# A selective scan on Trainium2: every second state's input term made tokens-first by ScalarE and turned by TensorE into PSUM

## The chip, the cores and the metric

One core of a Trainium2 chip runs the whole kernel. Its engines work side by side, each through its own queue in order: TensorE (PE; its weight loads are listed as PEld) multiplies matrices into PSUM, VectorE (DVE) and ScalarE (ACT) work element by element, GpSimd (POOL) issues the gathers, SyncE (SP) issues the other DMAs. The metric is the device time of one launch in microseconds (us).

## What is computed

Two layers on an image tensor of 4 x 128 x 128 x 128 (batch, height, width, channels), each added to its input after a group norm:

```
x = x + L0(gn(x))      # deformable convolution, two groups, nine taps
x = x + L1(gn(x))      # two Mamba blocks on rows of 128 tokens

def mamba_block(h):                      # d = 256 channels, n = 16 states
    u, res = split(h @ in_w)
    u      = silu(causal_conv4(u) + cb)
    dt, Bm, Cm = split(u @ xw)           # 8, 16, 16
    delta  = softplus(dt @ dtw + dtb)
    A      = -exp(A_log)
    # for every token t, channel d and state n:
    #   h[t] = exp(delta[t,d] * A[d,n]) * h[t-1] + delta[t,d]*u[t,d]*Bm[t,n]
    #   y[t,d] = sum_n h[t,d,n] * Cm[t,n]
    return ((y + u * Dp) * silu(res)) @ ow
```

The change concerns the recurrence over t alone: its decay `exp(delta*A)`, its input term `delta*u*B`, and the product with C. All is in 32-bit floats.

## The kernel before

Layer 0 (`layer0`, from line 420) gathers corners of a table with indirect DMAs (line 364, `gt`, four buffers), multiplies them by bilinear weights on VectorE (line 382, `gw`, two buffers), turns and sums them on TensorE into a bank `p4` of the pool `ps`, copies that to SBUF with ScalarE (line 396, `s`), and adds the taps up in PSUM (line 415, `acc`).

Layer 1 works on blocks of four sequences of 128 tokens (512 tokens), with channels on the partitions, 256 channels being NC = 2 tiles of 128. For each block and Mamba layer there are two parts:

- `pre` makes the projections: `u` (matmuls line 501 into two `ps1` tiles, Silu line 508), the gate `g` (513, 518), B, C and dt (`pdb` 521, `dbl` 524, sent to DRAM as `bcd` 526), then for each channel tile `pdt` (534), Abs, Exp, add and Ln on ScalarE (538 to 546) and two VectorE steps (547, 548) for softplus, and last `delta` (549) and `delta*u` (`du`, 550).
- `main` runs eight steps of two states (NQ = 2). A step broadcasts two rows of B and two of C to all partitions by DMA (570), clears the first column of each sequence's decays on ScalarE (575), makes four exponentials of 127 tokens in four sequences (580), multiplies `du` by B for each state (586, two products of 1024), runs one scan over 2 x 2 x 512 elements (592) that leaves the states in the decay tile `da` (three such tiles in turn), multiplies them by C (596, one product of 2048), and turns them on TensorE, adding into PSUM `y` (line 604, through the helper at 128). After the last step y is multiplied by the gate (607), turned back (`pyg`, 612, copied by 613) and projected (`pout`, 617 or 624 and 626, copied by 619 or 630).

`main` of a job is emitted after `pre` of the next job. Jobs go in the order block a layer 0, block b layer 0, block a layer 1, block b layer 1, then the next pair, so that the `pre` that runs under a `main` needs at most the output of the job before that `main`. There are 256 jobs. `u` has one buffer, so a `pre` can begin only when `main` of the job before it has started and read the old one (561).

The first image's layer 0 runs alone. Then a loop at the end (lines 661 to 668) deals out steps of layer 1 of one image and units of layer 0 of the next, and the last image's layer 1 runs alone. The order on each engine is set by a scheduler at compile time: it takes ready instructions in program order, a tile from a pool only when a buffer is free, and adds the semaphores. So the number of buffers of a pool shapes the order of every queue. PSUM has eight banks: `ps` 2, `psa` 2, `ps1` 2, and `y` 2.

The pools at lines 92 to 97 and `pre` and `main` are what the change touches. The helper that turns and adds is one line:

```
nc.tensor.matmul(o, v, ident, is_transpose=True, start=start, stop=stop, skip_group_check=True)
```

Of the kernel before, what the change touches and what calls it, by code (L numbers as in the profile page):

```python
# [10 lines left out]
F32 = mybir.dt.float32  # L11
# [6 lines left out]
P = 128  # L18
# [45 lines left out]
def block_kernel(ctx: ExitStack, tc: tile.TileContext, a: dict, out: bass.AP):  # L64
# [26 lines left out]
    pb = ctx.enter_context(tc.tile_pool(name="l0b", bufs=1))  # L91
    ps = ctx.enter_context(tc.tile_pool(name="l0ps", bufs=2, space=PSUM))
    psa = ctx.enter_context(tc.tile_pool(name="l0psa", bufs=2, space=PSUM))
    p2 = ctx.enter_context(tc.tile_pool(name="l1p2", bufs=1))
    pd = ctx.enter_context(tc.tile_pool(name="l1d", bufs=3, space=DRAM))
    ps1 = ctx.enter_context(tc.tile_pool(name="l1ps", bufs=2, space=PSUM))
    psy = ctx.enter_context(tc.tile_pool(name="l1psy", bufs=1, space=PSUM))

    def loadw(name, shape, src=None, pool=cw, tag=None):
        t = pool.tile(shape, F32, name=f"w_{name}", tag=tag) if tag else pool.tile(shape, F32, name=f"w_{name}")  # L100
        nc.sync.dma_start(t, a[name] if src is None else src)
        return t
# [32 lines left out]
    dw = loadw("dw", [P, NT, NT], pool=p2, tag="dbl")  # L135
    dwb = loadw("dwb", [P, NT], pool=p2, tag="ot")
    pw = loadw("pw", [P, NT, CG], pool=p2, tag="u")
# [19 lines left out]
    nc.vector.tensor_scalar(aneg, aneg, -1.0, None, ALU.mult)  # L157
    dpar = loadw("dpar", [P, NL, NC], pool=p2, tag="ot")
    for l in range(NL):
        for c in range(NC):  # L160
            nc.vector.tensor_scalar(ddiag[:, l, c, :], ident, dpar[:, l, c : c + 1], None, ALU.mult)
    inw = loadw("inw", [P, NL, NC * P], a["inw"][:, :, 0 : NC * P], pool=p2, tag="yg")
    cvw = loadw("cvw", [P, NL, DCONV, NC * P], pool=p2, tag="hs")
    for l in range(NL):
        nc.vector.tensor_tensor(
            inc[:, l], cvw[:, l], inw[:, l].unsqueeze(1).to_broadcast([P, DCONV, NC * P]), ALU.mult
        )
# [293 lines left out]

    NDA = 3
    das = [cw.tile([P, NC, NQ, SR, P], F32, name=f"da{i}") for i in range(NDA)]
    zero = cw.tile([P, NC * NQ * SR], F32, name="zero")
    nc.vector.memset(zero, 0.0)
    n_da = [0]
# [17 lines left out]
    def pre(st, l):  # L484
# [65 lines left out]
        nc.vector.tensor_tensor(du, de, u, ALU.mult)  # L550
        st.update(u=u, g=g, delta=de, du=du, bcd=bcd)

    def main(st, l):
# [5 lines left out]
        for i in range(SR):  # L559
            for c in range(NC):  # L560
                nc.tensor.matmul(  # L561
                    y[:, i, c], st["u"][:, c, i * P : (i + 1) * P], ddiag[:, l, c, :],
                    start=(i % 2 == 0 and c == 0), stop=False, skip_group_check=True,
                )
        for q in range(NS // NQ):
            bc = []
            for w in range(2):
                t = p2.tile([P, NQ, TB], F32, tag=f"bc{w}", name=f"bc{w}_{nm}_{q}", bufs=2)
                n0 = w * NS + q * NQ
                nc.sync.dma_start(t, st["bcd"][n0 : n0 + NQ, :].partition_broadcast(P))  # L570
                bc.append(t)
            da = das[n_da[0] % NDA]
            n_da[0] += 1

            nc.scalar.copy(da.rearrange("p c n s t -> p (c n s) t")[:, :, 0], zero)
            for c in range(NC):
                dv = st["delta"][:, c].rearrange("p (s t) -> p s t", s=SR)
                for n in range(NQ):
                    s = q * NQ + n
                    nc.scalar.activation(  # L580
                        da[:, c, n, :, 1:], dv[:, :, 1:], AF.Exp, scale=aneg[:, l, c, s : s + 1]
                    )
            hs = p2.tile([P, NC, NQ, TB], F32, tag="hs", name=f"hs_{nm}_{q}")

            for n in range(NQ):
                nc.vector.scalar_tensor_tensor(  # L586
                    hs[:, :, n, :], st["du"], ones[:, 0:1],
                    bc[0][:, n].unsqueeze(1).to_broadcast([P, NC, TB]),
                    op0=ALU.mult, op1=ALU.mult,
                )  # L590
            df = da.rearrange("p c n s t -> p (c n s t)")
            nc.vector.tensor_tensor_scan(  # L592
                df, df, hs.rearrange("p c n t -> p (c n t)"), zero[:, 0:1], ALU.mult, ALU.add
            )
            dc = da.rearrange("p c n s t -> p c (n s t)")
            nc.vector.scalar_tensor_tensor(  # L596
                dc, dc, ones[:, 0:1],
                bc[1].rearrange("p n t -> p (n t)").unsqueeze(1).to_broadcast([P, NC, NQ * TB]),
                op0=ALU.mult, op1=ALU.mult,
            )  # L600
            for c in range(NC):
                for n in range(NQ):
                    for i in range(SR):
                        add_transposed(y[:, i, c], da[:, c, n, i, :], False, q == NS // NQ - 1 and n == NQ - 1)
            yield
# [14 lines left out]
        else:  # L620
            x1t = load_x1(blk, f"o{nm}")
            for i in range(SR):
                o = po[:, i * P : (i + 1) * P]
                nc.tensor.matmul(o, x1t[:, i * P : (i + 1) * P], ident, start=True, stop=False)
                for c in range(NC):
                    nc.tensor.matmul(
                        o, yg[:, c, i * P : (i + 1) * P], ow[:, l, c, :], start=False, stop=(c == NC - 1)
                    )
            ot = p2.tile([P, SR, P], F32, tag="ot", name=f"ot_{nm}")
            nc.scalar.copy(ot.rearrange("p r c -> p (r c)"), po)  # L630
# [117 lines left out]
```

## Time and profile before

| what | value |
|---|---|
| median of three runs | 26672.16 us (26664.46 to 26679.19) |
| profiled execution, its own time | 26698.06 us |
| its span | 26696.0 us |
| busy: VectorE | 23505.8 us, 88% |
| busy: TensorE, weight loads | 19620.5 us, 73%; 13523.4 us, 51% |
| busy: GpSimd | 16017.0 us, 60% |
| busy: ScalarE | 11605.1 us, 43% |
| HBM traffic | 142 GB/s over the span |

A profile lists, for each engine, how long it was busy, in the whole span or in a stretch of it, and in groups of like instructions: line, engine, operation, output <- inputs, shapes and count, then busy time, mean duration of one in ns, and the idle time of the engine just before them with what ended it. A wait shown there is the engine's own: whoever stands behind it in its queue waits too. A share of the whole span mixes stages with different limits, so stages are read one by one.

### The profile page before, as it was taken

What the parts mean: (1) busy time and instruction counts of PE and PEld (TensorE: products, weight loads), DVE (VectorE), ACT (ScalarE), POOL (GpSimd) and SP (SyncE); (2) the same over time, 40 slices, a digit from 0 to 9 for tenths busy, and PEclk for the clock granted to TensorE, in tenths of its full rate; (3) what the DMA queues carried; (4) which work ended last, traced back from release to release, by engine and by line L of the source; (5) the groups of instructions that cost most, each with busy time, mean ns of one, the idle gap of its engine ahead of it and who ended that gap; (6) DMA issues with size and microseconds to landing.
All of it is one profiled execution on the core that took longest, in us unless ns stands there. A gap on an engine that the chain in (4) does not pass through costs nothing. (4 is left out here: it accounts for less than half of the span.)

```text
span 26696.0 us, 294801 instructions
## 1 busy us (share of the span) xinstructions
PE 19620.5 (73%) x112196; PEld 13523.4 (51%) x112196; DVE 23505.8 (88%) x14042; ACT 11605.1 (43%) x18181; POOL 16017.0 (60%) x9222
## 2 busy tenths in 40 slices
PE   4777788878888778887888778888888655555555
PEld 3444455555555555555555555555555443434344
DVE  2232289999999999999999999999999999999999
ACT  0000044444444544444444454444445455555554
POOL 4777777878877767888878667877878400000000
PEclk7888888888999888888998888899998866666666
DMA  5363344456544444455544444444444333333332
GB/s 146 114 172 107 106 147 155 157 170 183 165 153 154 149 144 155 158 173 181 164 154 153 148 143 151 156 150 152 154 154 156 130 107 106 107 106 107 107 106 102
DMA packets 1994602, 3804.53 MB, mean 143 GB/s; under 512 B 771796, under 2 KB 1116116, under 8 KB 1993053
## 3 DMA queue, kind: packets, MB, share of 16 engines
q1 hardware_dynamic: 1550812, 2577.13, 29.9%
q0 software_dynamic: 442368, 1208.55, 14.4%
q8 instruction: 880, 14.42, 0.2%
q14 instruction: 542, 4.43, 0.0%
HBM read 3567.63 MB, written 217.05 MB: 142 GB/s over the span
## 5 line engine op out<-in xcount | busy, mean ns | idle before, releaser
L364 POOL DMA_INDIRECT gt<-table,idx x9216 | 16016.3, 1738 | 5031.5 <-issue 2999.5
L592 DVE TENSOR_TENSOR_SCAN da<-da,zero,hs 128x2048 f32<-128x2048 f32 x2048 | 9176.1, 4481 | 351.7 <-ACT da L580 247.1
L128 PE MATMUL y<-ident,da 128*128 128x128 f32 x32768 | 5252.0, 326 | 3956.1 <-DVE da L596 3955.4
L580 ACT ACTIVATE da<-de,aneg 128x508 f32<-128x508 f32 x8192 | 5550.5, 712 | 5605.2 <-PE y L128 5351.0
L128 PEld LDWEIGHTS y<-ident,da 128*128 128x128 f32 x32768 | 4682.4, 171 | 4953.3 <-DVE da L596 2520.6
L415 PE MATMUL acc<-s,wc 128*64 128x256 f32 (+3 forms) x38400 | 6403.2, 453 | 761.4 <-ACT s L396 760.9
L586 DVE SCALAR_TENSOR_TENSOR hs<-du,ones,bc 128x1024 f32<-128x1024 f32 x4096 | 5093.2, 1277 | 0.0
L415 PEld LDWEIGHTS acc<-s,wc 128*64 128x64 f32 x38400 | 3352.0, 145 | 3083.2 <-issue 1446.2
L596 DVE SCALAR_TENSOR_TENSOR da<-da,ones,bc 128x2048 f32<-128x2048 f32 x2048 | 4807.9, 2348 | 25.9
L382 DVE TENSOR_TENSOR gw<-gt,wt 128x1024 f32<-128x1024 f32 x2304 | 2786.4, 1213 | 2133.3 <-DMA gt<-table,idx 1500.9
L128 PE MATMUL p<-ident,gw 128*128 128x128 f32 x18432 | 2724.3, 299 | 1714.1 <-DVE gw L382 1706.7
L128 PEld LDWEIGHTS p<-ident,gw 128*128 128x128 f32 x18432 | 2292.8, 154 | 2329.3 <-DVE gw L382 1752.7
L396 ACT COPY s<-p 128x512 f32<-128x512 f32 x1152 | 668.6, 581 | 3989.8 <-PE p L128 3982.0
L501 PE MATMUL pu<-hp,inc 128*128 128x512 f32 x4096 | 1808.3, 593 | 0.0
L580 ACT ACT_TABLE_LOAD x1016 | 1303.5, 1283 | 16.8 <-PE y L128 5.7
L501 PEld LDWEIGHTS pu<-hp,inc 128*128 128x128 f32 x4096 | 751.2, 188 | 865.9 <-issue 865.2
L508 ACT ACTIVATE u<-pu,w_cvb 128x512 f32<-128x512 f32 x512 | 324.6, 684 | 1468.9 <-PE y L561 1461.4
L561 PEld LDWEIGHTS y<-ddiag,u 128*128 128x128 f32 x4096 | 579.5, 200 | 192.0 <-issue 192.0
L612 PE MATMUL pyg<-ident,g 128*128 128x128 f32 x2048 | 353.9, 328 | 425.7 <-DVE g L607 424.8
L546 ACT ACT_TABLE_LOAD x500 | 641.5, 1283 | 8.9
L561 PE MATMUL y<-ddiag,u 128*128 128x128 f32 x4096 | 612.1, 284 | 0.0
L263 PE MATMUL pof<-xn,w_offw 128*64 128x512 f32 x2304 | 585.0, 613 | 20.0 <-ACT xn L257 12.0
(118 smaller groups left out, 11036.3 us busy)
## 6 DMA issues: line engine op xcount, KB each, us to landing
bc<-bcd SPq DMA_DIRECT2D x4096, 512.0 KB
gt<-table,idx POOLq DMA_INDIRECT x9216
table<-xt SPq DMA_DIRECT2D x984, 128.0 KB
xt<-in_x SPq DMA_DIRECT2D x124, 320.0 KB
xr<-in_x SPq DMA_DIRECT2D x128, 256.0 KB
x<-xo SPq DMA_DIRECT2D x128, 256.0 KB
x1t<-x SPq DMA_DIRECT2D x128, 256.0 KB
x1t_o<-x SPq DMA_DIRECT2D x128, 256.0 KB
```

What stands on the lines that cost most here:

```text
L128: nc.tensor.matmul(o, v, ident, is_transpose=True, start=start, stop=stop, skip_group_check=True)
L364: nc.gpsimd.indirect_dma_start(out=gt[:, v, r], out_offset=None, in_=flat, in_offset=bass.IndirectOffsetOnAxis(ap=idx[:, ri, o : o + 1], a ...
L382: nc.vector.tensor_tensor(gw.rearrange("p r s v c -> p (r s) v c"), gts[h].rearrange("p v r (s c) -> p (r s) v c", c=CG), wv.unsqueeze(3). ...
L396: nc.scalar.copy(st[:, :, 1 : W + 1], p4)
L415: nc.tensor.matmul(accs[b, j + i0][CG * g : CG * g + CG, q : q + rb - ra, :], wc[sl, v, e, :], st[p + 4 * g if p < 4 else 8][sl, ra:rb, kx ...
L501: nc.tensor.matmul(px.rearrange("p (s t) -> p s t", s=SR), inc[:, l, j, c * P : (c + 1) * P], h[:, :, j : j + P], start=(j == 0), stop=(j ...
L546: nc.scalar.activation(du[:, c], w1, AF.Ln)
L561: nc.tensor.matmul(y[:, i, c], st["u"][:, c, i * P : (i + 1) * P], ddiag[:, l, c, :], start=(i % 2 == 0 and c == 0), stop=False, skip_grou ...
L580: nc.scalar.activation(da[:, c, n, :, 1:], dv[:, :, 1:], AF.Exp, scale=aneg[:, l, c, s : s + 1])
L586: nc.vector.scalar_tensor_tensor(hs[:, :, n, :], st["du"], ones[:, 0:1], bc[0][:, n].unsqueeze(1).to_broadcast([P, NC, TB]), op0=ALU.mult, ...
L592: nc.vector.tensor_tensor_scan(df, df, hs.rearrange("p c n t -> p (c n t)"), zero[:, 0:1], ALU.mult, ALU.add)
L596: nc.vector.scalar_tensor_tensor(dc, dc, ones[:, 0:1], bc[1].rearrange("p n t -> p (n t)").unsqueeze(1).to_broadcast([P, NC, NQ * TB]), op ...
```

## The change

Every step's two states go two ways. The first is made as before, but in a tile of its own: B broadcast by DMA, a product of 1024 on VectorE, one scan of 1024 elements. For the second, `du` is turned once per `main` to tokens-first (`dut`: TensorE into `ps1`, ScalarE copies it out); there B of a state is one number per partition, which `pre` makes by turning `dbl` (`pbt`, `bt`). In each step ScalarE multiplies `dut` by it in four copies of 256 (`xs`, two tiles), TensorE turns these back into two PSUM banks (`px`, the new pool `psx`), one per channel tile, and VectorE scans each with 512 elements, reading its input term from PSUM.

Decays have one tile per state (`das`, four of them), cleared once: the exponentials never write the first column, and the scans no longer write into them but into `hs`, one of four tiles. The product with C is one of 1024 per state, in place. To make room in PSUM, `ps` and `ps1` go from two banks to one. SBUF tags are shared anew (`ot`, `cvw`, `dwb`, `dpar`).

```diff
-    ps = ctx.enter_context(tc.tile_pool(name="l0ps", bufs=2, space=PSUM))
+    ps = ctx.enter_context(tc.tile_pool(name="l0ps", bufs=1, space=PSUM))
...
-    ps1 = ctx.enter_context(tc.tile_pool(name="l1ps", bufs=2, space=PSUM))
+    ps1 = ctx.enter_context(tc.tile_pool(name="l1ps", bufs=1, space=PSUM))
+    psx = ctx.enter_context(tc.tile_pool(name="l1psx", bufs=2, space=PSUM))
...
-    NDA = 3
-    das = [cw.tile([P, NC, NQ, SR, P], F32, name=f"da{i}") for i in range(NDA)]
-    zero = cw.tile([P, NC * NQ * SR], F32, name="zero")
-    nc.vector.memset(zero, 0.0)
+    NDA = 4
+    das = [cw.tile([P, NC, SR, P], F32, name=f"da{i}") for i in range(NDA)]
+    for t in das:
+        nc.vector.memset(t, 0.0)
...
+        pbt = ps1.tile([P, SR, XP], F32, tag="t", name=f"pbt_{nm}")          # end of pre
+        for i in range(SR):
+            nc.tensor.transpose(pbt[:, i, :], dbl[:, i * P : (i + 1) * P], ident[0:XP, 0:XP])
+        bt = p2.tile([P, SR, NS], F32, tag="bt", name=f"bt_{nm}", bufs=2)
+        nc.scalar.copy(bt, pbt[:, :, DTR + 1 : DTR + 1 + NS])
...
+        dut = p2.tile([P, SR, NC * P], F32, tag="dut", name=f"dut_{nm}")       # start of main
+        for k in range(SR // 2):
+            pt = ps1.tile([P, 2, NC, P], F32, tag="t", name=f"pdu_{nm}_{k}")
+            for i in range(2):
+                for c in range(NC):
+                    o = (2 * k + i) * P
+                    nc.tensor.transpose(pt[:, i, c, :], st["du"][:, c, o : o + P], ident)
+            nc.scalar.copy(dut[:, 2 * k : 2 * k + 2], pt.rearrange("p s c d -> p s (c d)"))
         for q in range(NS // NQ):
...
+            bs = p2.tile([P, TB], F32, tag="bs", name=f"bs_{nm}_{q}", bufs=2)
+            nc.sync.dma_start(bs, st["bcd"][q * NQ : q * NQ + 1, :].partition_broadcast(P))
+            cs = p2.tile([P, NQ, TB], F32, tag="cs", name=f"cs_{nm}_{q}", bufs=2)
+            nc.sync.dma_start(cs, st["bcd"][NS + q * NQ : NS + q * NQ + NQ, :].partition_broadcast(P))
+            hs = [p2.tile([P, NC, TB], F32, tag="hs", name=f"hs_{nm}_{q}_{n}", bufs=4) for n in range(NQ)]
...
+                    nc.scalar.activation(d[:, c, :, 1:], dv[:, :, 1:], AF.Exp, scale=aneg[:, l, c, s : s + 1])
...
+            nc.vector.scalar_tensor_tensor(
+                hs[0], st["du"], ones[:, 0:1], bs.unsqueeze(1).to_broadcast([P, NC, TB]),
+                op0=ALU.mult, op1=ALU.mult,
+            )
+            h0 = hs[0].rearrange("p c t -> p (c t)")
+            nc.vector.tensor_tensor_scan(
+                h0, da[0].rearrange("p c s t -> p (c s t)"), h0, 0.0, ALU.mult, ALU.add
+            )
...
+            for i in range(SR):
+                nc.scalar.activation(xs[i // 2][:, i % 2], dut[:, i], AF.Copy, scale=st["bt"][:, i, s : s + 1])
             for c in range(NC):
+                px = psx.tile([P, SR, P], F32, tag="x", name=f"px_{nm}_{q}_{c}")
+                for i in range(SR):
+                    nc.tensor.transpose(px[:, i, :], xs[i // 2][:, i % 2, c * P : (c + 1) * P], ident)
+                nc.vector.tensor_tensor_scan(
+                    hs[1][:, c], da[1][:, c].rearrange("p s t -> p (s t)"), px.rearrange("p s t -> p (s t)"),
+                    0.0, ALU.mult, ALU.add,
+                )
             for n in range(NQ):
                 nc.vector.scalar_tensor_tensor(
+                    hs[n], hs[n], ones[:, 0:1], cs[:, n].unsqueeze(1).to_broadcast([P, NC, TB]),
                     op0=ALU.mult, op1=ALU.mult,
                 )
```

The two comments in the added lines are put in here to show where the lines stand; the turns of `hs` into `y` follow as before, eight per state.

## The prediction

> **What bounds the kernel now.** I read three views. First the page's row of VectorE by slices, and the busy time by stage (columns: length, then PE, PEld, DVE, ACT and POOL busy with counts, clock, DMA share, GB/s):
>
> ```profile
> DVE  2232289999999999999999999999999999999999
> 3400.00:21100.00 17700.00, 14206.85 (x83574) 9765.45 (x83570) 17247.06 (x10307) 8539.74 (x13461) 13633.95 (x6925) 0.89 0.49 157
> 21100.00:26696.00 5596.00, 2924.98 (x13261) 2241.90 (x13259) 5300.95 (x2608) 2823.85 (x4294) 0.00 (x0) 0.69 0.31 106
> ```
>
> After 3.4 ms of layer 0 alone (gather issues), VectorE is busy 97% while both layers run, and 95% at the end, where layer 1 is alone. The multiply of y by the gate (one per `main`) counts 188 up to 21.1 ms and 68 after: a `main`, "round" below, takes 17660/188 = 93.9 us in the shared stage (91.7 busy) and 82.2 in the last (78.0 busy). Next, what VectorE does in a step, and ScalarE's exponentials (groups by line: count, busy us, mean ns, idle before):
>
> ```profile
> L592 DVE TENSOR_TENSOR_SCAN da<-da,zero,hs 128x2048 f32<-128x2048 f32 x2048 | 9176.1, 4481 | 351.7 <-ACT da L580 247.1 <-PE pdt L534 11.2 <-DVE hs L586 3.3
> L580 ACT ACTIVATE da<-de,aneg 128x508 f32<-128x508 f32 x8192 | 5550.5, 712 | 5605.2 <-PE y L128 5351.0 <-DVE hs L586 48.7 <-DVE wn L303 36.0
> L586 DVE SCALAR_TENSOR_TENSOR hs<-du,ones,bc 128x1024 f32<-128x1024 f32 x4096 | 5093.2, 1277 | 0.0
> L596 DVE SCALAR_TENSOR_TENSOR da<-da,ones,bc 128x2048 f32<-128x2048 f32 x2048 | 4807.9, 2348 | 25.9
> ```
>
> The scan waited 0.35 ms in all: VectorE never needs anything late. A step is 2×1.277 + 4.481 + 2.348 = 9.38 us. TensorE only consumes here, so its delays are free.
>
> The third view is what the change touches without naming it: the chain that prepares the next round (`pre`). The first `pre` runs with nothing else on ScalarE (timeline, start and duration):
>
> ```profile
> 3440.06 7.71 PE L501 MATMUL pu<-hp,inc 128*128 128x512 f32 x16
> 3449.61 1.91 PE L521 MATMUL pdb<-u,w_xpw 128*41 128x512 f32 x4
> ...
> 3444.37 0.69 ACT L508 ACTIVATE u<-pu,w_cvb 128x512 f32<-128x512 f32 x1 [3.05 <-PE pu L501]
> 3447.80 0.69 ACT L508 ACTIVATE u<-pu,w_cvb 128x512 f32<-128x512 f32 x1 [2.75 <-PE pu L501]
> 3448.67 0.60 ACT L518 ACTIVATE g<-pr 128x512 f32<-128x512 f32 x1 [0.17 <-PE pr L513]
> 3451.55 0.68 ACT L524 ACTIVATE dbl<-pdb,w_xpb 41x512 f32<-41x512 f32 x1 [1.25 <-PE pdb L521]
> 3453.69 0.60 ACT L538 ACTIVATE e<-pdt 128x512 f32<-128x512 f32 x1 [1.46 <-PE pdt L534]
> 3454.31 1.28 ACT L539 ACT_TABLE_LOAD   x1
> ...
> 3463.52 1.22 DVE L550 TENSOR_TENSOR du<-de,u 128x1024 f32<-128x1024 f32 x1
> ```
>
> 24.7 us from the first `pu` matmul to the last `du`, with two banks of `ps1` overlapping neighbours. Before, this runs under eight steps of scans that do not need it.
>
> **The change, part by part.**
>
> *VectorE per step.* One product of 1024 goes (−1.277). The scan's 2048 elements become 1024+512+512. A split costs little: two products of 1024 cost 2×1.277 − 2.348 = 0.21 more than one of 2048; two of 512 (0.68) 0.09 more than one of 1024. Two splits: 4.481 + 0.3 = 4.8 (bounds 4.48 and 5.0). PSUM as source costs nothing: the line-548 product reads it in 682 ns, line 547 from SBUF 678. The product with C is split: 2.55. Sum 1.28 + 4.8 + 2.55 = 8.63, 0.75 less; 6.0 us a round, 1.53 ms over 2048 steps.
>
> *ScalarE per step.* The 0.21 us zero copy goes; four scaled copies of 256 come. Nearest rows: a plain copy of 260 takes 0.405, an exponential of 508 0.712; bounds 0.40 and 0.50, I take 0.47 (scaled like the latter): 4.5 us a step, beside 8.6 of VectorE.
>
> *TensorE per round.* 64 + 8 + 4 more transposes. Sixteen take 1.9 us when TensorE was busy, 3.65 after idling: 9 to 17 us on 14207/188 = 75.6, under any round length below.
>
> *SP and POOL.* SP issues two broadcasts a step as before, of three rows instead of four; nothing waited for them, so nothing is gained. POOL's queue holds gathers alone and none is moved past another.
>
> *Table loads.* The compiled order has 1554 instead of about 2030: 0.6 ms at 1.283 us off ScalarE, which is busy 48% of the shared stage and so hides it; those that stay stand in the chain below.
>
> *Inside steps the new wait is covered.* Scan and transposes alternate between two `px` banks: the first is freed 1.28 + 1.2 = 2.5 us into a step, refilled in some 0.7 us (four turns and a hop), and wanted 1.28 us into the next, at 9.9: about 6.7 us of slack for TensorE's queue. The copies for it must wait until the turns of the step before have read both `xs` tiles, 6.7 us into that step, and take 1.9: the same order of slack. What stands behind a waiting turn in TensorE's queue is y's turns (VectorE wants those a step later, for an `hs` buffer) and layer 0.
>
> *Between rounds it is not.* `dut`, from which the copies are made, is turned through `ps1`, now one bank, and stands after the next round's `pre` in the program. In the compiled order of the changed kernel this holds for every round with a `pre` behind it: TensorE does `pdu` after `pbt` of that `pre`, and VectorE meets (last stage, one round):
>
> ```
> hs0 product | hs0 scan | g | hs0 product with C | e, de of pdt 0 | e, de of pdt 1 | de | du | scan of px 0
> ```
>
> So from the last product of a round to the first `px` scan of the next, VectorE waits for the whole chain, and has 1.28+2.32+1.21+1.28 + 4×0.68 + 2.42 = 11.2 us to do. What stands behind it on ScalarE, the exponentials of the third step, is wanted later. The chain, last stage, from the rows: g behind a product and a half scan, 1.28 + 2.32 + 1.21 = 4.8 (y's last turns lie beside it); two `pyg` turns in series (1.15 to the copy at the kernel's end, copy 0.59), with `ddiag` matmuls between, 3.5; `pout` and copy 2.6 or 4.2, mean 3.4; `pu` to `dbl` 12.2 as shown, plus 2.5 because each of five fills now waits for the copy before it: 14.7; `pdt` 0: matmul 1.15, Abs 0.6, table load 1.28, Exp 0.63, add 0.62, two VectorE steps 1.4: 5.7, and only then `pdt` 1, which shared its load before: 4.3, then load and Ln 1.9, `bt` 0.3: 6.5; `pdu` 0.9, copies 1.2, four scaled copies 1.9, last turn 0.4: 4.4. Sum 43 us (bounds: 36 if dependent steps overlap as the independent ones in the rows do, 0.1 each, and the added waits vanish; 48 with 0.2 more per hop). Idle 43 − 11.2 = 32. A round is 78.0 − 6.0 + 32 = 104 instead of 82.2: 68 × 21.8 = +1.48 ms.
>
> *Shared stage.* VectorE has 8.3 of the 9.2 `gw` products of a round inside the window: 11.2 + 10.0 + about 1 of other layer-0 work = 22.2. The chain is longer: two `gw` stand ahead (2.4), and `s` copies and batches of line-415 matmuls sit between its links. Followed through one window: 50. Low bound 43 (all in gaps). High bound 58: a window with ten `gw` has four gathered ahead, six need 4 gathers each at 0.95 + 0.30 (median) to 1.98 + 0.30 us (stage mean), 30 to 55. I take 50, since scans that idle leave gathers near the median. Idle 28; round 91.7 − 6.0 + 28 = 113.7 against 93.9: 188 × 19.8 = +3.72 ms.
>
> *First stage.* POOL issues back to back, 740 gathers a ms at 1.04 + 0.30 us: one `p` bank less is hidden by that; bound +0.03 ms. I take 0.
>
> Sum against the profiled execution (26698; the median of 26672 is 26 lower): 26.70 + 1.48 + 3.72 = 31.90 ms, 31.87 on the median; I say 31.9.
>
> Two rules beside this. The Trainium skill's page "TensorE: Matmul & The Clock Gate" (HAM oscillation) reports that PSUM double-buffering gave a kernel no further gain; by that, halving the pools costs nothing and the sum would be 25.2 ms; the overlap in the `pre` rows speaks against it here. Its page "ScalarE: Activation LUTs" (Rules for kernel authors) asks to group activations by table set and budgets 2.7 us a switch; the rows have 1.28 us; with four exposed loads its figure would add some 5.7 us a round, 1.5 ms, for 33.4 ms.
>
> **The rivals.**
>
> *The cover holds (other side).* Only the 0.75 us a step count: 25.15 ms. That needs a chain shorter than VectorE's queued work, the 6.0 saved and the idle time already there: 11.2 + 6.0 + 4.2 = 21.4 us in the last stage, 30.4 in the shared. For it: 95% busy before. Against: `pre` alone took 24.7.
>
> *Steps stall too.* TensorE is in order, and in the shared stage a run of 46 line-415 matmuls took 6.68 us, about the slack of a `px` bank. At 1 us a step: 188 × 8 × 1 = +1.5 ms, 33.4; at 2 us 34.9. Against: the order spreads these runs in twos and threes between the turns.
>
> *Shorter windows.* At 36 and 43 us: idle 25 and 21; rounds 97 and 107: +1.0 and +2.4, 30.1 ms.
>
> **How the numbers follow.** Forecast 62%, steps stalling 18%, shorter windows 15%, cover holds 5%. A change of 0.2% is about what these runs can tell from none (they spread by 0.06%). Slower 0.95, same 0.01, faster 0.04. The range reaches from the short windows less 0.2 to stalls between 1 and 2 us: 29.9 to 34.3 ms.
>
> **What would show it.** Right: VectorE's share falls to about 75%; in groups, its largest idle stands before the half scans of line 617 of the changed kernel and the `pre` products, released by TensorE `px` or ScalarE; scans of 1024 near 2.3 us and of 512 near 1.2; the distance between gate products 104 us at the end. Wrong: half scans that wait in every step (second rival), round distances under 94 (first), a scan from PSUM well over 1.3 us, or a first stage longer than 3.5 ms.

## The result and the profile after

The changed kernel takes 31803.22 us, the median of 4 runs (31802.88 to 31809.3). The kernel before took 26675.67 us in the runs beside it (26664.46 to 26689.34). The ratio is 1.1922, with a 95% interval of 1.1902 to 1.1943: 5.1 ms slower. The forecast was 31.9 ms.

The page of the changed kernel first: VectorE's row by slices, then five of its groups.

```profile
DVE  2322577777777777777777777777777666666666
...
L384 DVE TENSOR_TENSOR gw<-gt,wt 128x1024 f32<-128x1024 f32 x2304 | 2783.5, 1220 | 4369.8 <-PE p L129 2429.4
L617 DVE TENSOR_TENSOR_SCAN hs<-da,px 128x512 f32<-128x512 f32 x4096 | 4880.6, 1203 | 696.5 <-PE px L616 696.5
L622 DVE SCALAR_TENSOR_TENSOR hs<-hs,ones,cs 128x1024 f32<-128x1024 f32 x4096 | 5062.4, 1271 | 0.2
L605 DVE TENSOR_TENSOR_SCAN hs<-da,hs 128x1024 f32<-128x1024 f32 x2048 | 4653.8, 2272 | 8.0 <-DVE hs L600 0.5
...
L549 DVE SCALAR_TENSOR_TENSOR e<-w,e 128x512 f32<-128x512 f32 x512 | 356.2, 696 | 4472.2 <-ACT w L547 4472.2
```

VectorE was at 9 in every slice of layer 1; now it stands at 7 and 6. Its idle time is not in the steps: the products with C (line 622) waited 0.2 us in all 4096 of them, the scans of 1024 (line 605) 8. It stands in front of line 549, the first VectorE step of the next round's `pre`, and in the shared stage in front of `gw`, whose `p` is late. The same by stage (length, then PE, PEld, DVE, ACT and POOL busy with counts, clock, DMA share, GB/s):

```profile
3400.00:26000.00 22600.00, 18047.72 (x100997) 12048.00 (x100993) 16564.01 (x13965) 11490.49 (x19280) 8124.18 (x6905) 0.88 0.35 109
26000.00:31800.00 5800.00, 3608.29 (x15092) 2601.15 (x15092) 3883.72 (x3030) 2958.35 (x4903) 0.00 (x0) 0.71 0.19 64
```

The gate products, one per round, date the rounds. The first comes at 3549.9 us (before: 3570.1), the 188th at 24626.8 (21011.2), the last at 31787.2 (26685.4). So a shared round takes 112.7 us instead of 93.3 and one of the last stage 105.3 instead of 83.4: 187 × 19.4 = 3.63 ms and 68 × 21.9 = 1.49 ms. With the 0.02 ms that the first stage gained, that is the whole difference of the two profiled executions, 31801.1 − 26696.0 = 5.1 ms.

Now a step and the turn of a round on VectorE, in the last stage (start, duration, and in brackets the idle time before):

```profile
28006.53 1.28 DVE L600 SCALAR_TENSOR_TENSOR hs<-du,ones,bs 128x1024 f32<-128x1024 f32 x1
28007.72 1.22 DVE L617 TENSOR_TENSOR_SCAN hs<-da,px 128x512 f32<-128x512 f32 x1
28008.85 2.27 DVE L605 TENSOR_TENSOR_SCAN hs<-da,hs 128x1024 f32<-128x1024 f32 x1
28011.04 1.20 DVE L617 TENSOR_TENSOR_SCAN hs<-da,px 128x512 f32<-128x512 f32 x1
28012.15 2.46 DVE L622 SCALAR_TENSOR_TENSOR hs<-hs,ones,cs 128x1024 f32<-128x1024 f32 x2
28014.52 1.28 DVE L600 SCALAR_TENSOR_TENSOR hs<-du,ones,bs 128x1024 f32<-128x1024 f32 x1
...
28022.51 1.28 DVE L600 SCALAR_TENSOR_TENSOR hs<-du,ones,bs 128x1024 f32<-128x1024 f32 x1
...
28054.90 0.69 DVE L549 SCALAR_TENSOR_TENSOR e<-w,e 128x512 f32<-128x512 f32 x1 [26.40 <-ACT w L547]
...
28061.71 0.69 DVE L549 SCALAR_TENSOR_TENSOR e<-w,e 128x512 f32<-128x512 f32 x1 [5.39 <-ACT w L547]
...
28069.19 2.33 DVE L617 TENSOR_TENSOR_SCAN hs<-da,px 128x512 f32<-128x512 f32 x2 [3.06 <-PE px L616]
```

The step runs without a pause and takes 14.52 − 6.53 = 7.99 us. The window, from the new round's first product, which VectorE takes ahead of the gate (22.51; the forecast calls it the last of a round), to the first scan of `px` (69.19), takes 46.7 us. Over all rounds it takes 50.8 us on average in the shared stage (VectorE busy for 21.3 of them) and 45.8 in the last (11.0). The idle time in it, 29.5 and 34.8 us, is all that VectorE has in a round. TensorE in the end of that window:

```profile
28056.37 2.07 PE L536 MATMUL pdt<-dbl,w_dtw 9*128 9x512 f32 x2 [4.74 <-DVE de L550]
28063.18 0.65 PE L556 MATMUL pbt<-ident,dbl 41*128 41x41 f32 x4 [4.74 <-DVE de L550]
28064.13 1.11 PE L580 MATMUL pdu<-ident,du 128*128 128x128 f32 x4 [0.30 <-ACT bt L558]
28065.92 1.12 PE L580 MATMUL pdu<-ident,du 128*128 128x128 f32 x4 [0.68 <-ACT dut L581]
...
28068.25 1.12 PE L616 MATMUL px<-ident,xs 128*128 128x128 f32 x4 [0.36 <-ACT xs L612]
```

`pdu`, whose input has been ready for a round, is turned only when `pbt` of the next job's `pre` has been read (`bt`). Each link waits for the copy out of the one `ps1` bank.

### The profile page after: what moved, and what is told of

The parts are those of the page before. It is cut to its first block, busy times and chain, and to the rows that moved or that the text cites. A ratio compares the mean times of both kernels' runs of the same rounds, so it can differ in the third digit from the quotient of the medians.

```text
span 31801.1 us, 348330 instructions
## 1 busy us (share of the span) xinstructions
PE 24073.4 (76%) x131652; PEld 16241.0 (51%) x131652; DVE 21421.8 (67%) x18141; ACT 14693.7 (46%) x24611; POOL 10491.8 (33%) x9222
## 4 chain that ended last, share of the span: by engine, by line
issue 30%; DVE 29%; PE 21%; POOL 14%; ACT 4%; DMA 2%; SPq 1%; DVEq 0%; POOLq 0%; ACTq 0%
POOL gt L366 14%; DVE hs L605 9%; DVE hs L617 6%; DVE hs L622 6%; PE acc L417 5%; DVE hs L600 5%; PE pu L503 4%; PE p L129 2%; DMA gt<-table,idx 2%; PE pdt L536 1%; PE pr L515 1%; PE y L569 1%; PE y L129 1%; PE pdb L523 1%; PE pdu L580 1%
## 5 line engine op out<-in xcount | busy, mean ns | idle before, releaser
L366 POOL DMA_INDIRECT gt<-table,idx x9216 | 10491.2, 1138 | 14155.8 <-DVE gw L384 11158.6
L129 PE MATMUL y<-ident,hs 128*128 128x128 f32 x32768 | 6032.3, 354 | 1560.2 <-DVE hs L622 1504.2
L129 PEld LDWEIGHTS y<-ident,hs 128*128 128x128 f32 x32768 | 5267.4, 187 | 2629.0 <-DVE hs L622 2285.5
L616 PE MATMUL px<-ident,xs 128*128 128x128 f32 x16384 | 3186.7, 325 | 3383.3 <-DVE hs L617 3312.7
L617 DVE TENSOR_TENSOR_SCAN hs<-da,px 128x512 f32<-128x512 f32 x4096 | 4880.6, 1203 | 696.5 <-PE px L616 696.5
L622 DVE SCALAR_TENSOR_TENSOR hs<-hs,ones,cs 128x1024 f32<-128x1024 f32 x4096 | 5062.4, 1271 | 0.2
L605 DVE TENSOR_TENSOR_SCAN hs<-da,hs 128x1024 f32<-128x1024 f32 x2048 | 4653.8, 2272 | 8.0 <-DVE hs L600 0.5
L616 PEld LDWEIGHTS px<-ident,xs 128*128 128x128 f32 x16384 | 2077.9, 162 | 4760.8 <-DVE hs L617 3160.9
L612 ACT ACTIVATE xs<-dut,bt 128x256 f32<-128x256 f32 x8192 | 3501.7, 496 | 153.8 <-PE px L616 125.5
L600 DVE SCALAR_TENSOR_TENSOR hs<-du,ones,bs 128x1024 f32<-128x1024 f32 x2048 | 2613.1, 1276 | 0.0
L503 PE MATMUL pu<-hp,inc 128*128 128x512 f32 x4096 | 1883.6, 601 | 45.8 <-ACT u L510 39.8
```

The source lines that it names most:

```text
L366: nc.gpsimd.indirect_dma_start(out=gt[:, v, r], out_offset=None, in_=flat, in_offset=bass.IndirectOffsetOnAxis(ap=idx[:, ri, o : o + 1], a ...
L503: nc.tensor.matmul(px.rearrange("p (s t) -> p s t", s=SR), inc[:, l, j, c * P : (c + 1) * P], h[:, :, j : j + P], start=(j == 0), stop=(j ...
L600: nc.vector.scalar_tensor_tensor(hs[0], st["du"], ones[:, 0:1], bs.unsqueeze(1).to_broadcast([P, NC, TB]), op0=ALU.mult, op1=ALU.mult,)
L605: nc.vector.tensor_tensor_scan(h0, da[0].rearrange("p c s t -> p (c s t)"), h0, 0.0, ALU.mult, ALU.add)
L612: nc.scalar.activation(xs[i // 2][:, i % 2], dut[:, i], AF.Copy, scale=st["bt"][:, i, s : s + 1])
L616: nc.tensor.transpose(px[:, i, :], xs[i // 2][:, i % 2, c * P : (c + 1) * P], ident)
```

## The experiments

The theory: the new turn (`pdu`, `dut`) takes its turn in `ps1` behind the next job's `pre`, and this opens the windows. The rivals: the halved bank counts by themselves; the steps; ScalarE's or TensorE's added work. The table has all runs: median, ratio to the kernel before, run beside it, with its interval, and the mean round in us between gate products of the profile, from the first to the 188th ("shared") and from there to the last ("last"). The kernel before has 93.3 and 83.4, the changed one 112.7 and 105.3.

| kernel | us | ratio | shared | last |
|---|---|---|---|---|
| e1 turn in its own `pre` | 26700.08 | 0.9999 (0.9989 to 1.0009) | 96.5 | 75.0 |
| e2 turn through `ps` | 27133.04 | 1.0163 (1.0146 to 1.018) | 98.6 | 75.4 |
| e3 before, `ps` and `ps1` one bank | 26578.74 | 0.9954 (0.9937 to 0.997) | 93.5 | 81.3 |
| e4 tiles per state, all on VectorE | 26599.07 | 0.9962 (0.9948 to 0.9976) | 93.7 | 80.8 |
| e5 e1, two `dut` | 26618.83 | 0.9977 (0.9968 to 0.9987) | 96.0 | 74.9 |
| e6 e1, `ps` two, `px` one bank | 27741.84 | 1.0399 (1.0381 to 1.0416) | 99.4 | 81.9 |
| e7 changed, `ps1` two, `px` one bank | 30691.55 | 1.1507 (1.1488 to 1.1527) | 109.2 | 98.8 |
| e8 e5, one group of sums out | 26445.88 | 0.9912 (0.9896 to 0.9929) | 95.1 | 74.9 |
| e9 half the turns in the shared stage | 26348.9 | 0.9876 (0.9859 to 0.9892) | 94.6 | 74.8 |
| e10 e5, no table loads | 26736.11 | 1.0013 (1.0003 to 1.0023) | 96.4 | 75.8 |
| e11 before, no table loads | 26411.59 | 0.989 (0.9873 to 0.9906) | 92.7 | 81.1 |
| e12 e5, four of nine sums out | 26219.24 | 0.9596 (0.958 to 0.9612) | 91.3 | 74.9 |

**e1: the turn at the end of its own job's `pre`.** The same instructions, pools and banks; the block only moves.

```diff
 def pre(st, l):
     ...
+    dut = p2.tile([P, SR, NC * P], F32, tag="dut", name=f"dut_{nm}")
+    for k in range(SR // 2):
+        pt = ps1.tile([P, 2, NC, P], F32, tag="t", name=f"pdu_{nm}_{k}")
+        ...
 def main(st, l):
-    dut = p2.tile([P, SR, NC * P], F32, tag="dut", name=f"dut_{nm}")
-    for k in range(SR // 2):
-        ...
```

> The changed kernel with one block moved: dut (the turned delta*u) is made at the end of the pre of its own job instead of at the start of its main, so that its two turns through the single ps1 bank come before the next job's pre and not after it. Same instructions, same pools. Theory (the time went into the window between rounds, opened by that order): the windows of 47 us close; the idle before the half scans and the pre products (about 35 us a round in the last stage) falls below 5, a round takes about VectorE's or TensorE's busy time (last stage 71 to 76 us, shared 83 to 92), in all 24.3 to 26.0 ms, below the kernel before. Rival A (the steps themselves, or the longer chain under single banks, cost the time wherever dut stands): 30 ms or more. Rival B (the single bank of ps holds up layer 0): last stage as in the theory, but shared rounds stay above 105 us, 29 ms or more.

It takes 26700 us: all 5.1 ms are gone, so the place of the turn in `ps1`'s order is the cause. The windows fall from 50.8 to 9.1 us in the shared stage and from 45.8 to 5.9 in the last, with VectorE busy for 8.1 and 4.7 of that. The last round is 75.0, below the 83.4 of before. But the shared round is 96.5, above the 93.3 of before, so the kernel is no faster: the expected 24.3 to 26.0 did not come. VectorE's waits between 3600 and 20800 us (total, count, longest):

```profile
DVE hs L618 <- PE px L617: 1062.5, 222, 17.9
DVE e L549 <- ACT w L547: 575.2, 149, 16.7
DVE gw L384 <- PE p L129: 452.6, 144, 12.0
```

These are rare and long, 2.1 of the 2.4 ms that VectorE idles there, and none is the per-step wait of the forecast's second rival.

**e2: the turn left in `main`, but through the sampling stage's pool.**

```diff
-            pt = ps1.tile([P, 2, NC, P], F32, tag="t", name=f"pdu_{nm}_{k}")
+            pt = ps.tile([P, 2, NC, P], F32, tag="t", name=f"pdu_{nm}_{k}")
```

> The changed kernel with one word changed: dut's two turns go through the bank of the pool ps (layer 0's) instead of that of ps1; their place in the program stays behind the next job's pre. Theory in its narrower form (the shared bank, not the place in the program, puts dut behind the next pre): the scheduler can then take the turns as soon as the old dut is read, the windows close, 24.3 to 26.5 ms. If the place in the program alone decides: as the changed kernel, 31.8 ms.

One word brings back 4.67 of the 5.1 ms; the 27.1 ms still lie above the expected 24.3 to 26.5. In the last stage, where nothing else uses `ps`, the round is within half a us of e1's. In the shared stage, where the turn has to share `ps` with the sampling tiles, it is 2.1 us worse than in e1, and VectorE's waits for `px` grow:

```profile
DVE hs L617 <- PE px L616: 1759.6, 253, 21.3
```

**e3: the kernel before with one bank in each of the two pools.**

```diff
-    ps = ctx.enter_context(tc.tile_pool(name="l0ps", bufs=2, space=PSUM))
+    ps = ctx.enter_context(tc.tile_pool(name="l0ps", bufs=1, space=PSUM))
-    ps1 = ctx.enter_context(tc.tile_pool(name="l1ps", bufs=2, space=PSUM))
+    ps1 = ctx.enter_context(tc.tile_pool(name="l1ps", bufs=1, space=PSUM))
```

> The kernel before with ps and ps1 cut from two banks to one each, nothing else. Theory: the longer chain stays hidden under the scans, since no scan of the running job needs ps1: 26.6 to 27.3 ms. Rival (single banks cost by themselves, on the pre chain or in layer 0): most of the 5.1 ms, 29 ms or more.

One bank each costs nothing; it even gains 0.46%, in the last stage (81.3 instead of 83.4). `pre` does get longer (from the first `pu` matmul to the last `du` 53 us instead of 43 in the shared stage and 38 in the last, medians), but this costs nothing as long as scans lie over it.

**e4: the other half of the change alone.** The decays and states in tiles per state, both products on VectorE, the banks as before, no `dut`, `xs`, `bt` or `px`.

```diff
+            for n in range(NQ):
+                nc.vector.scalar_tensor_tensor(
+                    hs[n], st["du"], ones[:, 0:1], bs[:, n].unsqueeze(1).to_broadcast([P, NC, TB]),
+                    op0=ALU.mult, op1=ALU.mult,
+                )
+            for n in range(NQ):
+                hn = hs[n].rearrange("p c t -> p (c t)")
+                nc.vector.tensor_tensor_scan(
+                    hn, da[n].rearrange("p c s t -> p (c s t)"), hn, 0.0, ALU.mult, ALU.add
+                )
```

> One part alone: decays and states in a tile per state (products and scans of 1024 each for both states, scans no longer in place, cleared columns), with pools of two banks as before and no ScalarE or TensorE path. The durations of the changed kernel's rows give 2 x 1.277 + 2 x 2.272 + 2 x 1.271 = 9.64 us a step. If instructions that do not depend on their neighbour follow it some 0.09 us early, as the changed kernel's rows do (its step is 7.99 us, its durations add up to 8.50), the step is about 9.1 and the kernel 26.1 ms. If not, 9.64 or more and 27.2 ms.

At 26.6 ms it gained less than the step promised. Splitting the scan is no cost but a small gain: the step falls from 9.39 to 9.15 us, though the same elements are covered by more instructions. VectorE in the last stage (a row with x2 is two instructions of one kind):

```profile
23999.25 2.47 DVE L587 SCALAR_TENSOR_TENSOR hs<-du,ones,bs 128x1024 f32<-128x1024 f32 x2
24001.64 4.46 DVE L593 TENSOR_TENSOR_SCAN hs<-da,hs 128x1024 f32<-128x1024 f32 x2
24006.02 2.45 DVE L597 SCALAR_TENSOR_TENSOR hs<-hs,ones,cs 128x1024 f32<-128x1024 f32 x2
24008.40 2.47 DVE L587 SCALAR_TENSOR_TENSOR hs<-du,ones,bs 128x1024 f32<-128x1024 f32 x2
```

Each group starts 0.08 us before the durations of the one ahead have run out. The step's gain is worth 8 × 0.24 = 1.9 us a round; the last stage shows 2.6, the shared one nothing (93.7 against 93.3).

**e7: the changed kernel with two banks for `ps1`, paid for with one of `px`.**

```diff
-    ps1 = ctx.enter_context(tc.tile_pool(name="l1ps", bufs=1, space=PSUM))
-    psx = ctx.enter_context(tc.tile_pool(name="l1psx", bufs=2, space=PSUM))
+    ps1 = ctx.enter_context(tc.tile_pool(name="l1ps", bufs=2, space=PSUM))
+    psx = ctx.enter_context(tc.tile_pool(name="l1psx", bufs=1, space=PSUM))
```

> The changed kernel (31,803 us), the turn left where the change put it, with two banks for ps1 (as before the change) and one for px. It tells apart the two halves of the cause: the bank shared with the next job's pre, and the place of the turn in the program. If the count of banks is what puts the turn behind the next job's pre, most of the 5.1 ms comes back, less what one px bank costs: 26.7 to 29 ms. If the turn in main is late however many banks there are, 31.5 to 33 ms.

Only 1.1 of the 5.1 ms come back, and the time lies between the two expectations. TensorE at the end of a window:

```profile
28038.00 1.98 PE L536 MATMUL pdt<-dbl,w_dtw 9*128 9x512 f32 x4 [0.77 <-ACT dbl L526]
28044.20 0.65 PE L556 MATMUL pbt<-ident,dbl 41*128 41x41 f32 x4 [4.22 <-DVE de L550]
28046.63 1.97 PE L580 MATMUL pdu<-ident,du 128*128 128x128 f32 x8 [1.79 <-ACT bt L558]
```

The two `pdt` run together, the chain is shorter, and `pdu` still comes after `pbt` and `bt`. The windows last 38.5 us in the last stage, where the changed kernel's last 45.8, and 45.3 in the shared one instead of 50.8. The lost `px` bank hides little of this: a step of the last stage takes 8.18 us instead of 7.99, 1.5 us a round. So it is the order in which tiles are taken from one pool, not the number of its banks, that puts `pdu` last: `pre` of the next job is written ahead of `main`. With e1 and e2 this settles the 5.1 ms: another place in the program, or another pool, ends all or most of it; a second bank shortens the windows but doesn't close them.

What was open from here is another question: why e1, with some 8 us less for VectorE to do in each round (83.2 busy instead of 91.1 in the shared stage), is not faster than the kernel before. Its last stage is (75.0 against 83.4); its shared stage is not.

**e5: two buffers for `dut` in e1.** (`e` and `x1t` keep one buffer each, for the space.)

```diff
-        dut = p2.tile([P, SR, NC * P], F32, tag="dut", name=f"dut_{nm}")
+        dut = p2.tile([P, SR, NC * P], F32, tag="dut", name=f"dut_{nm}", bufs=2)
```

> The kernel with the turn in its own job's pre (26,700 us), with two buffers for dut in place of one; e and x1t keep one buffer each in place of two, to pay for its space. In that kernel VectorE is busy 81-82 of about 96 us of a shared round. Between 3,600 and 20,800 us its idle time is 1,062 us before scans that wait for px (222 waits, mean 4.8), 575 us before e for ACT's w and 453 us before gw for p. Theory A: the one dut buffer ties the ends of two rounds together, since the next dut can be written only when the last scaled copy of the round has read this one. With two buffers most of the px waits go, and the w waits that follow from the same jam shrink: 24.6 to 25.8 ms. Rival B: TensorE, busy 85% there, sets the pace of the shared stage, and its queue finds other waits: 26.5 to 26.8 ms. If the single buffers of e and x1t cost more than the second of dut brings, above 26.8.

A gain of 0.5 us a shared round; theory A falls. The time is the one expected of rival B, TensorE's pace, which the next runs test. VectorE's three waits between 3600 and 20800 us stay almost as they were:

```profile
DVE hs L618 <- PE px L617: 1091.0, 243, 19.6
DVE e L549 <- ACT w L547: 606.2, 154, 16.7
DVE gw L384 <- PE p L129: 351.2, 137, 12.6
```

**e6: e1 with the banks dealt otherwise.**

```diff
-    ps = ctx.enter_context(tc.tile_pool(name="l0ps", bufs=1, space=PSUM))
-    psx = ctx.enter_context(tc.tile_pool(name="l1psx", bufs=2, space=PSUM))
+    ps = ctx.enter_context(tc.tile_pool(name="l0ps", bufs=2, space=PSUM))
+    psx = ctx.enter_context(tc.tile_pool(name="l1psx", bufs=1, space=PSUM))
```

> The kernel with the turn in its own job's pre (26,700 us), with the PSUM banks dealt otherwise: two for the sampling stage (ps), as before the change, and one for px in place of two. Theory: the sampling stage's waits for p (453 us in 3,600-20,800) go, but the second px of a step can only be turned once the first has been scanned, four transposes and a hop of some 1.3 us behind a scan of 1.2: if nothing stands between the two scans in VectorE's queue, +1.3 us for each of 2,048 steps, 2.7 ms, so 28.5 to 29 ms. Rival: the scheduler puts other work between the two scans, and the time is 26.2 to 26.9 ms.

27.74 ms lies between the two expectations. The second bank of `ps` brings `gw` little (its waits for `p` fall from 453 to 344 us), the missing one of `px` costs 7 us in every round of the last stage. Inside the round the compiled order puts other work between the two half scans, so that most steps run on, and stalls stand where it has too little, as here:

```profile
25000.42 1.26 DVE L601 SCALAR_TENSOR_TENSOR hs<-du,ones,bs 128x1024 f32<-128x1024 f32 x1
25004.04 1.22 DVE L618 TENSOR_TENSOR_SCAN hs<-da,px 128x512 f32<-128x512 f32 x1 [2.36 <-PE px L617]
```

So the two `px` banks earn their place, as the change had them.

**e8: half of the summing matmuls left out of e5.** One group of `add_up`, so half of the channels of that sum are not computed.

```diff
-                for g in range(G):
+                for g in range(1):
```

> The kernel with the turn in its own job's pre and two dut buffers (26,619 us), with half of the sampling stage's summing matmuls left out (one of the two groups in add_up, 19,200 of 38,400 matmuls, of 6,087 us busy). It is a test only: the second half of the channels of that sum is not computed. In that kernel TensorE is busy 86% and VectorE 87% between 3,600 and 20,800 us, and a shared round takes 96.5 us, with about 83 busy on each. Theory B of the run before, TensorE sets the pace there: three quarters of the summing fall in the shared stage, half of them are 12 us of each of its 188 rounds; the round falls to 85 to 87, 1.8 to 2.2 ms, with up to 0.4 ms more from the first stage: 24.0 to 24.9 ms. Theory C, the hops between engines at the turn of a round (px, w, p: waits of 5 us each that no one engine's load explains) set it: 26.0 to 26.6 ms.

0.65% less than e5. That lies in theory C's range, but it is neither theory's test, because TensorE was not relieved (busy 82.1 us of a shared round, 82.5 in e5). The group of the summing matmuls between 3600 and 20800 us, in e5 and then in this kernel (count, busy us, mean ns, idle before):

```profile
L417 PE MATMUL acc<-s,wc 128*64 128x256 f32 (+7 forms) x27240 | 4368.7, 427 | 179.0 <-ACT s L398 177.6
```

```profile
L417 PE MATMUL acc<-s,wc 128*64 128x256 f32 (+7 forms) x13774 | 4162.9, 438 | 120.2 <-ACT s L398 119.9
```

Half of the instructions took 95% of the time: the two groups had run side by side. They use separate halves of the array's columns (in the 64-row forms, a fifth of them, of its rows too). In e5 many of these matmuls start within 20 ns of the one before them, in e8 none within 100. The Trainium skill's page "TensorE: Matmul & The Clock Gate" (Part 3: Packing small matmuls, The mechanism) says that matmuls on separate tiles of the array run at the same time; these two rows agree.

**e12: four of the nine entries left out, for both groups.** That part of the sum is not computed.

```diff
-        for e in range(NT):
+        for e in range(0, NT, 2):
```

> The kernel with the turn in its own job's pre and two dut buffers (26,619 us), with four of the nine entries of add_up left out for both groups; a test only: that part of the sum isn't computed. It repairs the test with half of the sums, which didn't lighten TensorE: between 3,600 and 20,800 us it left out half of the summing matmuls, yet the time of that group went only from 4,369 to 4,163 us, since the two groups had run side by side. With five of nine entries the group should fall to some 2,430 us, 10.8 us less of a shared round of 95.9. If TensorE (82 of 95.9 us busy) sets the pace of the shared stage, the round falls to 85 to 88, 24.6 to 25.2 ms. If it is the order of the queues and their hand-overs, with neither engine's load, the round stays at 94 or more: 26.2 to 26.6 ms. In between (25.3 to 26.1), the two engines share it.

It takes 26219.24 us, a ratio of 0.9596 to a kernel before that took 27317.65 beside it, 2.4% more than beside the others. This kernel's own first stage was also 0.52 ms longer than e5's (first gate product at 4052.5 instead of 3534.7 us; the cause is not known), so it is read by its rounds: 91.3 shared, 74.9 last. Now TensorE was relieved:

```profile
L417 PE MATMUL acc<-s,wc 128*64 128x256 f32 (+6 forms) x15424 | 2842.9, 447 | 367.1 <-ACT s L398 312.0 <-issue 48.4 <-ACT du L548 3.0
```

Per round the group falls from 4368.7 × 96.0/17200 = 24.4 to 2842.9 × 91.3/17200 = 15.1 us, TensorE's whole busy time by less, from 82.5 to 75.6, and the round by 4.7. Half to two thirds of what is taken off TensorE comes back as time: it shares the pace of the shared stage, the middle one of the three cases. VectorE's waits for `px` and `w` shrink with it, to a third of e5's in sum:

```profile
DVE hs L618 <- PE px L617: 483.8, 167, 15.3
DVE e L549 <- ACT w L547: 105.7, 59, 6.2
```

**e9: a version that beats both kernels.** e5's turn in `pre` (one `dut`); up to block 94, about the shared stage, the odd `q` make both products on VectorE (a product and a scan of 1024, as for `hs[0]`), so that ScalarE and TensorE serve every fourth state there and every second in the last stage.

```diff
+            if blk < 94 and q % 2:
+                b1 = p2.tile([P, TB], F32, tag="b1", name=f"b1_{nm}_{q}", bufs=2)
+                ...
+            else:
                 s = q * NQ + 1
                 ...
```

> A version meant to share the load between the engines: the turn in its own job's pre, and in the first 188 rounds (the shared stage) only every fourth state's product is made by ACT and turned, the others on VectorE; in the last 68 every second, as in the changed kernel. dut keeps one buffer. If TensorE and VectorE together set the pace of the shared stage, its round lies between the 96.5 us of all the turns and the 93.9 of none, or below both, since each engine has some slack: VectorE 83.5 plus four times 1.2 is 88, TensorE 83 less 32 transposes of 0.18 is 77; 91 to 93 us, so 25.4 to 26.3 ms with the last stage's 75.4. If the hops between engines set it, they are there with half of the turns too, and the round stays at 95 or more: 26.4 to 26.7 ms.

26349 us, 1.2% below the kernel before and 17% below the changed one. VectorE has 4.3 us a round more to do in the shared stage than in e5, yet the round is 1.4 shorter: with all the turns in place, more is lost elsewhere than VectorE saves. TensorE is busy 79.4 us of the round instead of 82.5, ScalarE 55.2 instead of 60.5; this run does not tell their shares apart. The time lies just above the 25.4 to 26.3 expected of a full sharing of the load.

**e10 and e11: no table loads,** in e5 and in the kernel before. Identity stands for Silu and Ln, so these functions are not computed.

```diff
-            nc.scalar.activation(u[:, c], px, AF.Silu, bias=cvb[:, l, c : c + 1])
+            nc.scalar.activation(u[:, c], px, AF.Identity, bias=cvb[:, l, c : c + 1])
-            tc.keep_in_program_order(nc.scalar.activation(g[...], px, AF.Silu))
+            tc.keep_in_program_order(nc.scalar.activation(g[...], px, AF.Identity))
-            nc.scalar.activation(du[:, c], w1, AF.Ln)
+            nc.scalar.activation(du[:, c], w1, AF.Identity)
```

> The kernel with the turn in its own job's pre and two dut buffers (26,619 us), with Identity in place of Silu (u and g) and of Ln (du) on ACT: a test only, the activation functions are left out so that ACT never changes its table. The kernel has some 9.3 table loads of 1.283 us in a shared round, 12 us of ACT; at the turn of a round ACT runs for 44 us without a pause over 1 us, with 13 loads among it, and that is where VectorE waits for px and w. Theory D, ACT's queue at the turn of the round sets how much of the shorter steps is kept: VectorE's 13 idle us of a shared round fall to 2 to 6, the round from 96.5 to 86 to 90: 24.7 to 25.5 ms. Rival: the waits are those of queues in a fixed order, each engine late in turn, and stay whatever ACT's load: 26.2 to 26.6 ms.

> The control to the run before: the kernel before the change with the same three functions left out of ACT. VectorE is busy 97.7% in its shared stage, with ACT at 48%, so neither theory gives the loads a price here: 26.4 to 26.7 ms.

Theory D falls clearly, and e10's 26.74 ms lie even above its rival's range. ScalarE loses 12 us of a shared round and the round grows by 0.4. The waits only change places: fewer before `px`, more before `w` and `p`.

```profile
DVE e L549 <- ACT w L547: 858.2, 145, 18.4
DVE hs L618 <- PE px L617: 740.5, 236, 17.1
DVE gw L384 <- PE p L129: 592.3, 168, 13.9
```

In the kernel before the same edit gains 1.1%, somewhat more than half of it in the last stage (83.4 to 81.1).

What stays open: VectorE is busy 83 us of e5's shared round of 96.0. TensorE's load accounts for a part of the other 13, as e12 shows; ScalarE's table loads and the single `dut` buffer are excluded. That the rest is the order of the queues, each engine late in turn, is argued, not shown: each of the edits from e5 on also changed the compiled order, and none changed the order alone.

## Why the prediction was right

**The sign and the cause.** Right, and for the reason given. The windows at the turn of a round are there in the trace and hold all of VectorE's idle time in a round, e1 closes them and the 5.1 ms go with them, and e2 and e7 show that it is the turn's place in `ps1`'s order. One sign was misplaced: the idle time was forecast before the half scans and the `pre` products; it stands nearly all before the latter and before `gw`, and the half scans waited 0.7 ms. VectorE's share, forecast at about 75%, is 74% of a shared round and 67% of one of the last.

**The shared stage, +3.72 ms, and the last, +1.48.** Measured +3.63 and +1.49. (The forecast's own base, 93.9 and 82.2, put the edge between the stages elsewhere; by gate products it is 93.3 and 83.4.) The sum hides two terms that missed in opposite directions.

**VectorE per step, 8.63 us.** Mis-sized: it is 7.99. The durations were forecast well (1.276, 2.272, 2 × 1.203, 2 × 1.271; sum 8.50), with the scan's two splits at 0.2 instead of 0.3. The step that failed is adding durations and taking the old step's 9.38 as their sum. Neighbours that do not depend on each other overlap: six starts a step, each 0.085 us early. In the kernel before, a scan right behind its own product and a product with C right behind its own scan each start late. VectorE there, in steps with nothing else between them, in the last stage:

```profile
24000.13 2.47 DVE L586 SCALAR_TENSOR_TENSOR hs<-du,ones,bc 128x1024 f32<-128x1024 f32 x2
24002.73 4.48 DVE L592 TENSOR_TENSOR_SCAN da<-da,zero,hs 128x2048 f32<-128x2048 f32 x1
24007.25 2.35 DVE L596 SCALAR_TENSOR_TENSOR da<-da,ones,bc 128x2048 f32<-128x2048 f32 x1
24009.52 2.48 DVE L586 SCALAR_TENSOR_TENSOR hs<-du,ones,bc 128x1024 f32<-128x1024 f32 x2
```

The scan starts 0.13 us and the product with C 0.04 us after the end of what it reads; the next step's product, which depends on neither, 0.08 us before the product with C has ended. The split lets the scheduler put another state's work between a scan and its product. Such a step becomes 1.40 us shorter, nearly twice the 0.75 forecast. Not all of that counts, since in the kernel before other work stood between most scans and their neighbours: only some 800 of the 2048 follow right behind their product. Over whole rounds VectorE's busy time falls from 91.1 to 83.2 us in the shared stage and from 79.2 to 70.5 in the last, where 6.0 were forecast: 2.1 ms in all instead of 1.53.

**The chain of 43 us in the last stage.** 46.7 in the window shown and 45.8 on average, above the forecast, inside its bound of 48. Link by link: gate 4.8 (4.8 forecast), `pyg` 3.8 (3.5), `pout` 4.1 (3.4), `pu` to `dbl` 15.3 (14.7), `pdt` 0 5.9 (5.7), `pdt` 1 to `bt` 7.8 (6.5), `pdu` to the scan 5.1 (4.4). The largest miss is the second `pdt`. A round idles 34.8 us instead of 32. In the shared stage the window takes 50.8 where 50 were forecast from following one, with 7.4 `gw` products in it instead of 8.3, and a round idles 29.5 us instead of 28.

These two misses cancel, and that they do is luck: VectorE's work per round came out at 83.2 and 70.5 us instead of 85.7 and 72.0, its idle time 1.5 and 2.8 longer. Each is worth some half a ms.

**ScalarE's scaled copies at 0.47, bounds 0.40 and 0.50.** 0.496, at the upper bound, and hidden within steps.

**PSUM as a source costs the scan nothing; steps do not stall.** Right as far as the rows tell: 1.203 us a half scan, where a line through the scans of 1024 and 2048 elements (2.272 and 4.481) would give an estimate of 1.17; no run scans 512 from SBUF. All the waits for `px` are 696 us, 229 of them of about 3 us, all but one at the end of a window. The second rival is refuted: the two `px` banks cover the steps, as e6 shows by taking one away.

**The cover holds (25.15 ms).** Refuted for the changed kernel. But e1, where the cover does hold, is at 26.7, not 25.15: its last round is what this rival says (75.0 against 82.2 − 6.0 = 76.2), its shared round is not (96.5 against 87.9). The forecast gave TensorE's added work no price as long as it is below the round; e12 shows that it has one in the shared stage.

**The two rules.** The one kernel for which double-buffered PSUM gave no further gain (the Trainium skill's page "TensorE: Matmul & The Clock Gate", HAM oscillation) was set against the overlap in the `pre` rows. For `ps` and `ps1` by themselves it is so here too: e3 loses nothing with single banks. For `px` it is not: one bank costs 1.04 ms (e6 against e1). The forecast's conclusion held for another reason, the turn's place among the tiles of one pool. For table switches the budget of 2.7 us (the Trainium skill's page "ScalarE: Activation LUTs", Rules for kernel authors) doesn't fit: a load in the trace takes 1.28, and from the end of the activation before it to the start of the next there are 1.31 us (median).

## What to carry to other kernels

Here a new tile taken from an existing pool queued behind every tile that is written ahead of it there, those of prefetched work too: look up what is written between its input and its first reader, and move it before that work or give it another pool; a second bank brought back only 1.1 of 5.1 ms here. An engine's share of busy time only says that it has work; what shorter steps of one engine are worth is read stage by stage, at the hand-overs: 8 us less for VectorE made e1's last round 8.4 us shorter and its shared round 3.2 us longer. When a step is priced, read it from start to start in the timeline, not as a sum of durations.

## What the runs showed of the hardware that was not expected

On VectorE an instruction that doesn't depend on its neighbour starts some 0.08 us before the neighbour's recorded end, and one that does starts 0.04 to 0.13 us after it (in the kernel before, medians: a product right behind another 0.081 before, a product with C right behind its scan 0.036 after, a scan right behind its product 0.105 after); two scans of 1024 elements (4.46 us from the first start to the last end) are no dearer than one of 2048 (4.48).

Leaving out half of the 64-column matmuls on TensorE saved 5% of their time, because their partners had run beside them; leaving out four ninths of both saved 38% a round. TensorE was busy 86% between 3600 and 20800 us in e5, and still 86% in e8 with 13,500 matmuls fewer.

Taking every table load out of ScalarE, 12 us of a round of 96, changed the time by 0.4% in the wrong direction in e5, while in the kernel before it gained 1.1%.
